# Two graph-attention layers over neighbour lists: the second layer in source order, two more row buffers, and other distances between the stages

## The chip, the cores and the metric

The kernel runs on one core of a Trainium2 chip. Its engines work beside each other, each on a queue of its own, and meet at semaphores: TensorE (PE, with its weight loads as PEld), VectorE (DVE), ScalarE (ACT), GpSimd (POOL) and SyncE (SP). POOL and SP issue the DMA transfers. The metric is the device time of one execution in microseconds (us). A profile is taken of one execution by the hardware profiler.

## The reference, cut to what matters

Two layers, each a graph attention with a residual and a layer norm. There are 8 graphs (the batch) of 2048 nodes with 256 features; all share one adjacency matrix, in which a node has 5 to 36 neighbours, itself among them.

```python
# layer 0: dot-product attention
h1, h2, h3 = x @ W1, x @ W2, x @ W3
e = leaky_relu(h1 @ h2.T, 0.2)                 # per graph, 2048 x 2048
e = where(adj > 0, e, -1e12)
x = layernorm(x + relu(softmax(e) @ h3))
# layer 1: additive attention, 4 heads of 64
q = x @ W
e = leaky_relu(q . a_src [i] + q . a_dst [j], 0.2)   # per head
e = where(adj > 0, e, -9e15)
x = layernorm(x + elu(softmax(e) @ q))
```

## The kernel before, in words

**Sparse form.** The 2048 nodes are sorted by their number of neighbours and cut into 16 tiles of 128 nodes. Tile `t` has a fixed number of neighbour slots, `SLOTS[t]`, from 36 down to 12 (596 in all). Of each tile a list of neighbour numbers is made (`neighbours`): the adjacency row, in which each entry holds its column number or 0, is cut into 24 blocks, `nc.vector.max` takes the eight largest of each block, and rounds of `max` and `match_replace` take the largest eight of what is left, until the tile's slots are filled. The lists are good if no block holds more than eight neighbours of a node; a flag is computed from the counts (`checks`), and a general path is run if it is set.

**Units.** The batch is worked in two halves of four graphs. A unit is one layer, one half and one tile; there are 64, first the 32 of layer 0 (each half from the tile of 12 slots up to that of 36), then the 32 of layer 1 (with the tile of 36 in the middle of each half). For each slot POOL gathers 128 rows, one per node, by an indirect DMA (`gather`, L203): in layer 0 from the inputs (4096 B per row: four graphs), in layer 1 from a table of projected rows that layer 0 stored (`qg`, 4160 B per row with the logit terms). Two slots make a chunk, which lies in one row buffer; there are 16 (`RING`).

**Layer 0.** `own_rows` gathers the unit's own nodes into the one buffer `xo`; `before0` copies them by four SP transfers into a residual buffer (`xr`, four of them), turns them on PE and projects them (`g`, two buffers). `logits0` takes, for each slot and graph, one fused multiply and sum on DVE (L594). Then come a softmax over the slots, diagonal matrices of the weights on ACT (`diagonals`, L723), and PE adds the rows with these as weights (`add_slot`, L706). A unit of 16 slots or more is split into two parts, each with its own softmax; the second takes the first's maximum and sum along (an online rescale). `after0` projects the sum by `W3`, adds the residual (`residual`, L778), normalises, and stores both the result and the table row for layer 1.

**Layer 1.** `logits1` adds the two logit terms per chunk (L879), `sums1` multiplies the gathered rows by the weights in place (`weighted`): four chunks of five on DVE (L943), the fifth in 32 small pieces on ACT (L939). PE sums them with a unit matrix. A unit over 24 slots, which is the tile of 36 alone, is split in two; here each part has its own maximum, and `shares` and `after1` combine both at the end (L970, L976). `after1` then makes the elu, the residual, the layer norm and scatters four blocks of rows by POOL (L211).

**What sets the order.** `tick` is called once for each slot summed, and where a stage has to wait for another. Each call advances a clock and lets every stage put a little into the queues: own rows, row gathers as far as row buffers are free (`pump`, `credits`), what has been put down for this time by `due`, diagonals up to `AHEAD` slots before the sums, and dots or adds (`stream`) up to a limit of slots before the sums. In layer 0 that limit is the slots of the next part plus `SLACK` = 9; in layer 1 it is those, plus what is left of this part, plus `LEAD` = 5. `starts`, `ends` and `lists` are queues of generators that are advanced two steps per call. For layer 0 the queues of DVE, ACT and PE are exactly in this order (`ordered`). For layer 1 that is ended (`ordered.__exit__` at unit 32), and the framework's planner orders those three engines by its own estimates of durations; POOL's order is by hand throughout, and SP's is the planner's.

**Buffers.** Sums lie in four PSUM buffers (`acc_tile`), two per part; `wide_tile` has four buffers for turned and projected rows.

Of the kernel before, what the change touches and what calls it, by code (L numbers as in the profile page):

```python
# [24 lines left out]
P = 128  # L25
# [15 lines left out]
RING = 16  # L41

SPLIT = 16
LEAD = 5
LATE = 6
SLACK = 9
AHEAD = 2

BLOCKS = 24
# [86 lines left out]
def fast_path(  # L136
# [39 lines left out]
    ring = ctx.enter_context(tc.tile_pool(name="ring", bufs=RING))  # L176
    xop = ctx.enter_context(tc.tile_pool(name="xown", bufs=1))
    xrp = ctx.enter_context(tc.tile_pool(name="xres", bufs=4))
    gp = ctx.enter_context(tc.tile_pool(name="g", bufs=2))
    wp = ctx.enter_context(tc.tile_pool(name="wide", bufs=4))  # L180
    qp = ctx.enter_context(tc.tile_pool(name="q", bufs=1))
    hsp = ctx.enter_context(tc.tile_pool(name="hs", bufs=1))
# [49 lines left out]

    twice = const.tile([P, 64], F32, tag="twice", name="twice")
# [14 lines left out]
    meta = gp.tile([P, NT, 8], F32, tag="g", name="meta")  # L248
# [4 lines left out]
    junk = hsp.tile([P, N], BF16, tag="hs", name="junk")  # L253
# [132 lines left out]
    def statistics(y, name):  # L386


        st = sp.tile([P, 2, nc.vector.BN_STATS_DIM], F32, tag="st", name=f"st_{name}")
        for i in range(2):  # L390
            nc.vector.bn_stats(st[:, i, :], y[:, 2 * i : 2 * i + 2, :].rearrange("p b c -> p c b"))  # L391
            yield
        mv = st.rearrange("p i (b s) -> p (i b) s", s=3)
        return mv[:, :, 1], mv[:, :, 2]

# [53 lines left out]
    class Unit:  # L449
        def __init__(self, layer, h, t):  # L450
# [10 lines left out]
            self.chunks = [[] for _ in self.parts]  # L461
            self.p = [None] * len(self.parts)
# [46 lines left out]
    def neighbours(t):  # L509
# [12 lines left out]
        some = sp.tile([P, 8 * BLOCKS], F32, tag="some", name=f"some_{t}", bufs=1)  # L522
        for i in range(BLOCKS):
            nc.vector.max(some[:, ts(i, 8)], v[:, N * i // BLOCKS : N * (i + 1) // BLOCKS])
            if i % 8 == 7:
                yield
# [17 lines left out]
    def own_rows(u):  # L544
        u.xo = xop.tile([P, HC], F32, tag="xo", name=f"xo_{u.name}")
        gather(u.xo, xg[u.h][:, :], order[:, u.t : u.t + 1])

    def before0(u):
# [18 lines left out]
        u.g = gp.tile([P, HC], F32, tag="g", name=f"g_{u.name}")  # L567
# [56 lines left out]
    def weights0(u, i, K, e, m):  # L624
# [7 lines left out]
        if i == len(u.parts) - 1:  # L632
# [5 lines left out]
            if i:  # L638
                due(2, spread_shares, u, e)
# [3 lines left out]
    def spread_shares(u, e):  # L643

        fs = sp.tile([P, 2, 2], F32, tag="f0", name=f"f0_{u.name}", bufs=2)
        for r in range(2):
            rr = slice(64 * r, 64 * r + 64)
            pf = ps_tile(f"ps_f0_{u.name}_{r}")[:, :2]
            for c in range(2):
# [3 lines left out]
                    rhs=e[rr, ts(c, 2), 0],  # L653
# [6 lines left out]

    def shares(u, G):


        f = sp.tile([P, 2, HG], F32, tag="f", name=f"f_{u.name}", bufs=1)[:, :, :G]
        top = sp.tile([P, HG], F32, tag="top", name=f"top_{u.name}", bufs=1)[:, :G]
        nc.vector.tensor_tensor(top, u.m[0], u.m[1], ALU.max)
        for i in range(2):
            nc.vector.tensor_tensor(f[:, i, :], u.m[i], top, ALU.subtract)
        nc.scalar.activation(f, f, AF.Exp)
        for i in range(2):  # L670
            nc.vector.tensor_tensor(u.s[i], u.s[i], f[:, i, :], ALU.mult)
        nc.vector.tensor_tensor(top, u.s[0], u.s[1], ALU.add)
        nc.vector.reciprocal(top, top)
        nc.vector.tensor_tensor(f, f, top.unsqueeze(1).to_broadcast([P, 2, G]), ALU.mult)
        fs = sp.tile([P, 2, 2, HG // 2], F32, tag="fs", name=f"fs_{u.name}", bufs=1)
        fs = fs[:, :, :, : G // 2]
        for r in range(2):
            rr = slice(64 * r, 64 * r + 64)
            pf = ps_tile(f"ps_f_{u.name}_{r}")[:, :G].rearrange("p (i g) -> p i g", i=2)
            for c in range(2):  # L680
                nc.tensor.matmul(
                    pf[64 * c : 64 * c + 64],
                    lhsT=ident[rr, rr],
# [733 lines left out]
```

## Time and profile before

| | |
|---|---|
| median of three runs | 2350.33 us (2346.8 to 2351.26) |
| the profiled execution: its time, its span | 2346.12 us, 2344.4 us |
| DVE busy | 2043.6 us (87%) |
| PE busy (weight loads) | 1714.5 us (959.1) |
| POOL busy | 1527.7 us (65%) |
| ACT busy | 1439.8 us (61%) |
| DMA | 734.95 MB, mean 313 GB/s |

A line of a group reads: line of the kernel, engine, operation, what is written and read (program names), shape, count, then busy time and the mean duration of one in ns, then the time in which the engine stood idle just before them, and what ended that. A line of waits gives the engine and line that waited, what released it, the sum in us, how often, and the longest. A line of the timeline gives start and duration in us, then the instruction, and in brackets the idle time before it and its releaser. "issue" means that the profile shows no release by another engine.

### The profile page before, as it was taken

The numbers are of one execution on the slowest core, as the hardware profiler recorded it, in microseconds if no ns is written. First come the engines' busy times: TensorE is split into PE (matmuls) and PEld (weight loads), VectorE is DVE, ScalarE is ACT, GpSimd is POOL, SyncE is SP. The second block draws the span as 40 slices with busy tenths as digits, with TensorE's granted clock in tenths as the row PEclk, the third lists the DMA queues.
The fourth block names the chain that finished last, engine by engine and source line by source line (L and its number), as shares of the span: only waits on it lengthen the run. The fifth ranks groups of instructions, "written<-read, shape, count | busy, mean of one in ns | idle before, by whom it ended". The sixth has DMA issues, their size and how long they took to land. (4 is left out here: it accounts for less than half of the span.)

```text
span 2344.4 us, 52672 instructions
## 1 busy us (share of the span) xinstructions
PE 1714.5 (73%) x16835; PEld 959.1 (41%) x16835; DVE 2043.6 (87%) x7238; ACT 1439.8 (61%) x4951; POOL 1527.7 (65%) x1485
## 2 busy tenths in 40 slices
PE   0237798898788989999998877565655776665664
PEld 0125565566455656766665532122211222222222
DVE  6587899999999987999999597888887888998996
ACT  5316577676677767888886864442564656543545
POOL 3355466665666655766776667776777777775773
PEclk9659999999999999999999988787878888887887
DMA  9877799998896889999998689978999999977992
GB/s 386 290 256 263 263 353 343 341 329 302 311 347 209 287 286 308 361 344 332 342 367 320 239 291 329 352 269 310 343 352 354 350 341 376 353 272 287 364 333 83
DMA packets 249420, 734.95 MB, mean 313 GB/s; under 512 B 63200, under 2 KB 72544, under 8 KB 246704
## 3 DMA queue, kind: packets, MB, share of 16 engines
q0 software_dynamic: 192512, 645.89, 76.4%
q1 hardware_dynamic: 55360, 84.44, 10.8%
q8 instruction: 137, 2.24, 0.4%
q10 hardware_dynamic: 1264, 1.18, 0.2%
q14 instruction: 147, 1.20, 0.1%
HBM read 708.35 MB, written 76.09 MB: 335 GB/s over the span
## 5 line engine op out<-in xcount | busy, mean ns | idle before, releaser
L594 DVE CUSTOM_DVE_ANT_0 j<-s,g 128x256 bf16<-128x256 f32 x2384 | 846.9, 420 | 57.0 <-DMA s<-xg,idx 56.4
L203 POOL DMA_INDIRECT s<-xg,idx x596 | 632.7, 1062 | 392.4 <-issue 126.8
L706 PE MATMUL acc<-s,ident 64*64 64x512 f32 x4768 | 608.9, 663 | 334.4 <-issue 277.2
L203 POOL DMA_INDIRECT s<-qg,idx x596 | 606.2, 1017 | 224.2 <-issue 132.5
L706 PE MATMUL acc<-s,dg 64*64 64x256 f32 x9536 | 632.4, 393 | 108.2 <-ACT dg L723 107.9
L723 ACT ACTIVATE dg<-twice,e 128x64 f32<-128x64 f32 x2384 | 604.4, 341 | 34.2 <-PE acc L706 16.2
L943 DVE TENSOR_TENSOR s<-s,p 128x2048 f32<-128x2048 f32 (+1 forms) x260 | 574.4, 2230 | 0.0
L706 PEld LDWEIGHTS acc<-s,ident 64*64 64x64 f32 x4768 | 209.4, 149 | 729.2 <-issue 577.6
L706 PEld LDWEIGHTS acc<-s,dg 64*64 64x64 f32 x9536 | 363.1, 136 | 334.9 <-ACT dg L723 183.2
L939 ACT ACTIVATE s<-s,e 128x64 f32<-128x64 f32 x1408 | 342.7, 335 | 47.1 <-DVE e L909 37.9
L594 DVE DVE_READ_ACCUMULATOR2_ANT e<- 128x1 f32 x2384 | 194.3, 81 | 0.0
L211 POOL DMA_INDIRECT out_dram<-o,oidx x128 | 128.7, 1006 | 68.5 <-ACT o L418 32.5
L400 ACT ACTIVATE z<-st,roots 128x4 f32<-128x4 f32 x64 | 19.0, 297 | 236.6 <-DVE st L391 202.1
L879 DVE TENSOR_TENSOR e<-s,own 128x32 f32<-128x32 f32 (+1 forms) x306 | 55.9, 186 | 104.5 <-DMA s<-qg,idx 101.9
L818 PE MATMUL ps_q<-wqs,x1T 128*128 128x264 f32 x512 | 133.4, 404 | 14.9 <-DVE y L778 14.9
L440 PE MATMUL ps_p_g<-A,xT 128*128 128x256 f32 x512 | 122.7, 393 | 1.7 <-DVE y L778 1.7
L440 PE MATMUL ps_p_h<-w_sb,hT 128*128 128x256 f32 x512 | 120.4, 388 | 2.0 <-DVE e L879 2.0
L818 PEld LDWEIGHTS ps_q<-wqs,x1T 128*128 128x128 f32 x512 | 94.1, 193 | 51.1 <-DVE y L778 17.5
L418 ACT ACTIVATE o<-xr,nmr,rstd 128x256 f32<-128x256 f32 x128 | 66.5, 589 | 75.1 <-DVE nmr L414 73.3
L1064 ACT COPY q<-ps_q 128x264 f32<-128x264 f32 x128 | 47.4, 377 | 104.1 <-PE ps_q L818 101.0
L440 PEld LDWEIGHTS ps_p_g<-A,xT 128*128 128x128 f32 x512 | 97.3, 195 | 26.3 <-issue 9.6
L440 PEld LDWEIGHTS ps_p_h<-w_sb,hT 128*128 128x128 f32 x512 | 95.1, 191 | 26.9 <-issue 14.4
(143 smaller groups left out, 1489.9 us busy)
## 6 DMA issues: line engine op xcount, KB each, us to landing
adj<-in_adj_dram SPq DMA_DIRECT2D x16, 1024.0 KB
xr<-xo SPq DMA_DIRECT2D x128, 128.0 KB
x1s<-y SPq DMA_DIRECT2D x32, 512.0 KB
xr<-x1s SPq DMA_DIRECT2D x32, 512.0 KB
s<-xg,idx POOLq DMA_INDIRECT x596
s<-qg,idx POOLq DMA_INDIRECT x596
edges<-adj SPq DMA_DIRECT2D x16, 512.0 KB
xg<-in_x_dram SPq DMA_DIRECT2D x4, 2048.0 KB
```

The costliest lines, as they stand in the source:

```text
L203: nc.gpsimd.indirect_dma_start(out=dst, out_offset=None, in_=table, in_offset=AT(ap=index, axis=0), bounds_check=table.shape[0] - 1, oob_i ...
L211: ins = nc.gpsimd.indirect_dma_start(out=table, out_offset=AT(ap=index, axis=0), in_=src, in_offset=None)
L418: nc.scalar.activation(dst[:, b, :], y[:, b, :], AF.Identity, bias=nmr[:, b : b + 1], scale=rstd[:, b : b + 1],)
L440: nc.tensor.matmul(pp[:, ts(j, C)], lhsT=srcT[:, ts((2 * i + j) * KC + k, P)], rhs=weight[:, k, :], start=(k == 0), stop=(k == KC - 1),)
L594: nc.vector.tensor_tensor_reduce(out=jt, in0=rows[:, s, ts(b, C)], in1=u.g[:, ts(b, C)], scale=1.0, scalar=0.0, op0=ALU.mult, op1=ALU.add, ...
L706: nc.tensor.matmul(out, lhsT=lhsT, rhs=rhs, start=(k == 0 and j == 0), stop=(k == K - 1 and (j == 1 or diag is None)), tile_position=(64 * ...
L723: nc.scalar.activation(diag[:, b, :], twice, AF.Copy, scale=u.p[i][:, b, k : k + 1])
L818: nc.tensor.matmul(pq[:, : C + 2 * H], lhsT=u.x1T[:, ts(i * KC + k, P)], rhs=w.sqs[:, k, j * H : j * H + CD + H], start=(k == 0), stop=(k ...
L879: nc.vector.tensor_tensor(e[:, c * CHUNK : c * CHUNK + ns, :].rearrange("p s (b g) -> p s b g", b=HB), rows[:, :ns, :].rearrange("p s (b w ...
L939: nc.scalar.activation(v[:, a, g, :], v[:, a, g, :], AF.Copy, scale=pv[:, a, g : g + 1])
L943: nc.vector.tensor_tensor(v, v, pv.unsqueeze(3).to_broadcast([P, n * HB, H, D]), ALU.mult)
L1064: heappop(events)[2]()
```

## The change

- *Lists:* the adjacency row is cut into 16 blocks for tiles of more than 19 slots and into 12 for the others, where it was 24; the rounds after that read 128 or 96 values where they read 192.
- *Row buffers:* the ring has 18 buffers. Two are held through layer 0 (`held`): one holds both `g` buffers, the other `xo` and `hs`, whose own pools are gone. They join the ring when the last table row of layer 0 has been put into POOL's queue.
- *Own rows:* a unit's own rows are gathered once the unit five before it has had its residual (`rested`), where it was at the start of the unit three before it. `before0` and `before1` of a unit start at the begin of the unit three before it, where it was in its middle.
- *Lead:* in layer 0 the dots may lead by at least 22 slots (`LEAST`); the limit was 17 to 21 for most split units. In layer 1 the limit is the slots of the next part plus 6.
- *Layer 1 in source order:* `ordered` ends after the last unit. Softmax, multiplies and ends are put down with `due` at fixed distances (`maxima1`, `weights1`, `scaled`, `share_of_first`, `after1`); the multiplies lead the sums by about two slots, the ACT pieces are spread over eight calls. A split unit is rescaled online as in layer 0: `share_of_first` scales the first part's sum after four slots of the second.

```diff
+MORE = 2
-LEAD = 5
-SLACK = 9
+SLACK = (9, 6)
+LEAST = (22, 0)
...
-    ring = ctx.enter_context(tc.tile_pool(name="ring", bufs=RING))
-    xop = ctx.enter_context(tc.tile_pool(name="xown", bufs=1))
+    ring = ctx.enter_context(tc.tile_pool(name="ring", bufs=RING + MORE))
-    gp = ctx.enter_context(tc.tile_pool(name="g", bufs=2))
-    hsp = ctx.enter_context(tc.tile_pool(name="hs", bufs=1))
...
+    held = [ring_tile(f"held_{i}") for i in range(MORE)]
+    g_rows = held[0][:, : 2 * HC].rearrange("p (i c) -> p i c", i=2)
+    xo_rows, hs_rows = held[1][:, :HC], held[1][:, HC : 2 * HC]
...
-        for i in range(BLOCKS):
-            nc.vector.max(some[:, ts(i, 8)], v[:, N * i // BLOCKS : N * (i + 1) // BLOCKS])
+        blocks = 16 if K > 19 else 12
+        for i in range(blocks):
+            nc.vector.max(some[:, ts(i, 8)], v[:, N * i // blocks : N * (i + 1) // blocks])
             if i % 8 == 7:
                 yield
...
+                if u.layer == 1:
+                    yield from scaled(u, i, K)
+                    continue
...
+    def scaled(u, i, K):
...
+        for c in range(chunks):
+            if c % SHARE == 0 and c + SHARE - 1 < chunks:
+                for a in range(operands(c + SHARE - 1, u.ps[i])[0]):
+                    due(a, by_columns, c + SHARE - 1, a)
+            n, v, pv = operands(c, u.p[i])
+            if c % SHARE != SHARE - 1:
+                nc.vector.tensor_tensor(
+                    v, v, pv.unsqueeze(3).to_broadcast([P, n, H, D]), ALU.mult
+                )
+            u.done[i] = c + 1
+            yield n // HB
...
+                rested[0] += 1
                 due(2, roots)
...
             tabled[0] += 1
+            if tabled[0] == 2 * NT:
+                credits[0] += MORE
...
+    def maxima1(u, i, k0, K, e):
...
+        if i:
+            nc.vector.tensor_copy(e[:, 0, :], u.m[0])
...
+        due(1, nc.scalar.activation, v, v, AF.Exp)
+        due(3, weights1, u, i, K, e)
...
+    def share_of_first(u):
+        u.v = wide_tile(f"v_{u.name}")[:, :HC]
+        for r in range(2):
+            nc.vector.tensor_tensor(
+                u.v[:, ts(r, HW)].rearrange("p (a d) -> p a d", d=D),
+                u.accs[0][r].rearrange("p (a d) -> p a d", d=D),
+                u.fs[:, r, :].unsqueeze(2).to_broadcast([P, HG // 2, D]),
+                ALU.mult,
+            )
...
+            for k in range(K):
+                c, s = divmod(k, CHUNK)
+                while u.done[i] <= c:
+                    yield 0
...
+                add_slot(acc, k, K, rows[:, s, :], None)
+                if s == n - 1:
+                    credits[0] += 1
+                if i == 1 and k == 4:
+                    share_of_first(u)
+                yield 1
...
+        at = 4 if split else 2
+        due(2, whole)
+        due(at, exponentials)
+        due(at + 1, below)
+        due(at + 4, less)
+        due(at + 5, above, 0)
+        due(at + 6, above, 1)
...
-        if m < min(opened[0] + 4, 2 * NT) and (m == 0 or units[m - 1].turned):
+        if m < min(rested[0] + 5, 2 * NT) and (m == 0 or units[m - 1].turned):
...
-        if j == 2 * NT:
-            ordered.__exit__(None, None, None)
...
+        if j + 3 < len(units):
+            v = units[j + 3]
+            starts.append(before[v.layer](v))
...
-            drawn[0] -= share if u.layer == 0 else 0
+            drawn[0] -= share
...
-            tick(follow[i] + (SLACK if u.layer == 0 else left - ends_of[i] + LEAD))
-            if not begun and left <= u.K / 2 and j + 3 < len(units):
...
+            tick(max(follow[i] + SLACK[u.layer], LEAST[u.layer]))
+        (after0, after1)[u.layer](u)
...
+    ordered.__exit__(None, None, None)
```

## The prediction

> **What bounds the kernel now.** I read the stage table first, then the groups by line, then what GpSimd (POOL) and VectorE (DVE) wait for in each stage, and last the order of time at the places where they stop. The profiled execution took 2346.1 us (span 2344.4); the three timed runs have a median of 2350.3, 4.2 us above it.
>
> The stage table has, per window: length, then busy time of PE, PEld, DVE, ACT and POOL, PE clock, DMA share, GB/s. Setup ends near 120, layer 0 near 1300, and the gathers of layer 1 end at 2292.
>
> ```profile
> 120.00:300.00 180.00, 115.36 (x1120) 77.39 (x1122) 149.06 (x789) 82.54 (x290) 94.16 (x89) 0.83 0.75 262
> 300.00:780.00 480.00, 418.62 (x4640) 281.29 (x4632) 464.30 (x2521) 340.19 (x1228) 306.10 (x290) 0.96 0.91 315
> 780.00:960.00 180.00, 168.22 (x1852) 117.62 (x1854) 147.93 (x789) 136.63 (x481) 107.61 (x104) 0.97 0.90 304
> 960.00:1300.00 340.00, 321.70 (x3740) 219.25 (x3736) 332.67 (x1774) 273.06 (x998) 230.96 (x218) 0.98 0.94 335
> 1440.00:2292.00 852.00, 533.14 (x4180) 182.56 (x4184) 741.17 (x997) 436.89 (x1513) 635.47 (x628) 0.81 0.91 333
> ```
>
> In layer 0 DVE is the bound: 464 of 480 and 333 of 340 us busy. It idles 31 us in 120 to 300 and 32 us in 780 to 960, where the second half of the batch begins. In layer 1 DVE is busy only 741 of 852 us. POOL's busy time, 635 of 852, looks lower, but its rows show the truth:
>
> ```profile
> 1447.35 0.99 POOL L203 DMA_INDIRECT s<-qg,idx  x1 [0.30 <-issue]
> 1448.64 0.99 POOL L203 DMA_INDIRECT s<-qg,idx  x1 [0.31 <-issue]
> ...
> 1631.66 1.44 POOL L203 DMA_INDIRECT s<-qg,idx  x1 [9.44 <-PE acc L706]
> ...
> 2151.19 0.99 POOL L203 DMA_INDIRECT s<-qg,idx  x1 [13.78 <-PE acc L706]
> ```
>
> A gather costs 0.99 us and a gap of 0.30 behind it whatever happens, 1.29 us in all, and they follow each other without a wait. 628 x 1.29 = 810 of the 852 us: POOL issues without pause, and DVE waits for it. Of what it waits for in this window
>
> ```profile
> POOL s L203 <- PE acc L706: 30.2, 25, 13.8
> DVE e L879 <- DMA s<-qg,idx: 77.7, 55, 3.4
> ```
>
> 25 waits for a free row buffer make 30.2 us, and two of them, 9.44 and 13.78, make 23.2 of it; the other 23 average 0.3, which is the gap. Both large ones follow a tile of 36 slots, the only one split in layer 1. PE shows why:
>
> ```profile
> 1627.05 18.63 PE L706 MATMUL acc<-s,ident 64*64 64x512 f32 x144 [22.93 <-issue]
> ...
> 2146.58 13.99 PE L706 MATMUL acc<-s,ident 64*64 64x512 f32 x104 [25.89 <-issue]
> ```
>
> PE stands for 22.9 and 25.9 us: a split unit holds all four sum buffers until its end combines them on DVE (L970), the next unit has none, and no rows are freed.
>
> **The change part by part.**
>
> *Lists.* Today a list takes 24 MAX8 of 85 or 86 columns, then rounds over 192 values.
>
> ```profile
> 107.90 3.60 DVE L524 MAX8 some<-nb 128x8 f32<-128x85 int16 x24
> ...
> L524 DVE MAX8 some<-nb 128x8 f32<-128x85 int16 x256 | 49.7, 231 | 0.0
> L531 DVE MAX8 m<-some 128x8 f32<-128x192 f32 x44 | 15.7, 356 | 0.3
> L533 DVE MATCH_REPLACE8 some<-m,some 128x192 f32<-128x192 f32 x28 | 9.6, 343 | 0.0
> ```
>
> From 231 ns at 85 to 356 at 192 is 1.17 ns a column. Eight in a row take 1.28 us, 160 ns each, since they overlap; so 210 ns at 128 columns and 261 at 171. A list is 3.84 us now, 16 x 0.210 = 3.36 after for the five tiles over 19 slots, 12 x 0.261 = 3.13 for the other eleven: 5 x 0.48 + 11 x 0.71 = 10.2 us. The rounds read 128 or 96 values instead of 192, 75 or 112 ns less: 29 of the 72 rounds and replacements belong to the large tiles, 43 to the others, 2.2 + 4.8 = 7.0. Together -17, all on DVE in the first half of layer 0, where it is the bound. The ends are 0 (the DMA share of 0.91 takes over) and -20.
>
> There is also one pause less or two in making a list. In 120 to 300 POOL stands five times for 10.6 to 13.4 us, each time before the first row gather of a unit, which needs its list; DVE waits 33.7 us for rows there. A pause is a slot of about 2 us, and the list is 1 us shorter: 5 x 3 = 15 us on POOL. I take -6, since DVE has other rows to work on for part of it; ends -15 and 0.
>
> *Own rows.* Before, POOL gathers them at the start of a unit, and its queue stands until the copies of the previous own rows (SP) have found a free residual buffer.
>
> ```profile
> 835.80 1.01 POOL L203 DMA_INDIRECT xo<-xg,order  x1 [8.80 <-DVE e L594]
> ...
> 844.28 0.43 DVE L594 CUSTOM_DVE_ANT_0 j<-s,g 128x256 bf16<-128x256 f32 x1 [4.87 <-DMA s<-xg,idx]
> ```
>
> Row gathers are queued behind, and DVE goes dry 8 us later; the same pair comes at 892 and 901 (6.34, then 4.52). After, the gather is put behind the residual that frees the buffer. -9 (4.87 + 4.52). At best the 8.45 us at 934, where DVE waits for a projection, goes too: -18. At worst PE, which now turns own rows some two slots after their gather in units of 12 or 13 slots, waits for the landing: four units by 2 to 3 us, +10. POOL issues and SP copies stay 32 and 128.
>
> *Lead of 22 slots and the earlier start of a unit.* The lead was 17 to 21 for most units that are split. Nothing is added; dots are moved ahead. With 32 slots of rows, those in flight fall from about 15 to 10, some 19 us of DVE against the 2.6 us that a chunk takes to issue and about 4 to land (the shortest distance from the last issue to the add that had waited for it is 4 us). I take 0. DVE idles 16 + 7 us in the stages where this acts: -16 at best. If rows run late as in 120 to 300, +25.
>
> *Layer 1 in source order.* The online rescale takes the place of the combination at the end for the two split units. The first part is scaled after four slots of the second, which frees two sum buffers before the next unit asks. Both POOL waits go: -(9.44 + 13.78 - 2 x 0.30) = -23; the other end is 0, if the next wait in line is as long. The DVE work of unsplit units (L943 at 2.28 us, adds, softmax, end) is the same; for split ones it falls by a few us, beside POOL's issues: 0. If that cover were gone, the 741 us of DVE would be the floor.
>
> What the order itself does I take as 0. An add (L879) now stands in DVE's queue with the multiplies behind it, and PE and POOL's buffers wait for those. A gap hidden until now is DVE's 111 us, of which 78 are waits for gathers. A source order that puts no add before its rows have landed gains nothing either, as POOL is the bound; at most the 20 us of buffer waits in 1300 to 1440 (25.1 less 17 gaps) go. Its bad end is the rival below.
>
> Here a rule of the Trainium skill gives another sum. Perfetto Trace Analysis, section Identifying the Most-Contended Engine, takes the engine with the highest occupancy as the one to work on, for VectorE and GpSimd alike. By it DVE (741) is ahead of POOL (635), and its idle 111 us would be what a better order can win: -111 for this part, and 2200 in all. The rows of 1447 decide against that, since POOL's gap of 0.30 us is not counted as busy and yet can't be used. Another section of that page, What "DMA-bound" means, speaks against the part in the way the rows do: where the issuing engine's track is solid DMA instructions, that engine is the bound, and no order of the other three changes it.
>
> *Two more row buffers.* They come with the last table rows, which POOL stores at 1420. After that, waits for buffers other than the two are at the gap: 0; at best part of the same 20 us.
>
> *The tail.* After the last gather (2292.4) the ends of three units follow one another. PE stands 9.06 us at 2309 for a sum buffer, and the last exponentials start 4.7 us after PE is done (2323.0, 2327.7).
>
> ```profile
> 2309.43 13.60 PE L706 MATMUL acc<-s,ident 64*64 64x512 f32 x96 [9.06 <-DVE xr L989]
> ```
>
> In source order the end of the third last is over by then, but about two chunks of the last but one are multiplied after the last adds (4.6 us): -4, ends -14 and +5.
>
> **Sum.** -17 - 6 - 9 + 0 - 23 + 0 - 4 = -59. 2346.1 - 59 = 2287; the median is mostly a little above the profiled execution, so 2288.
>
> **The rivals.**
>
> *Half of it:* one of the layers keeps its time. In layer 0 the DMA share (0.91 to 0.94) speaks for it, the 98% of DVE against it. Without layer 0's 32 us it is 2320, without layer 1's 27 us 2315. 0.20.
>
> *More of it:* the pauses at the begin of each half of layer 0 (31 + 32 us) close by two thirds instead of a quarter, 27 more, and the 20 us between the layers by half: 2288 - 37 = 2251. All of them are waits in a queue for something issued late, which is what is moved. 0.12.
>
> *Slower: adds that wait at the head of DVE's queue.* Place: L879 in layer 1, some 290 adds of two slots. POOL's solid time in that window is 852 - 23 = 829 us, DVE's work 741: waits of 88 us fit, 0.30 us an add; today's are 0.27. Beyond, the window lasts 741 us and the waits. At 0.51 us an add (147 us) it lasts 36 us longer than now, which is the gain elsewhere (32 + 4); at 0.6 us (174) it is 741 + 174 - 852 - 36 = +27: 2377. For it: adds now come 4 to 10 us after the issue, with 4 needed, so a fixed order has little room. Against it: at 20 slots a unit has 36 - 26 = 10 slots (15 us) between the issue and the add. 0.16.
>
> *No change:* the order loses in layer 1 what layer 0 gains: 2350. 0.04.
>
> **How the numbers follow.** My case has 0.48 with its own range 2265 to 2308. Faster: 0.48 + 0.20 + 0.12 = 0.80; same, within 0.2% (about what a measurement of this kernel can tell from no change, 4.7 us): 0.04; slower: 0.16. The range leaves out the slower case and the far end of the fast one: 2240 to 2345.
>
> **What would show it.** Right: no MAX8 of 85 columns, DVE in 300 to 780 still at 97% and the end of layer 0 some 32 us earlier; own-row gathers that wait under 2 us; PE without a stop over 10 us behind the 36-slot tiles, POOL at 1.29 us per gather with no wait over 3 us; at most 45 us from the last gather to the end. Wrong: POOL's waits for row buffers in layer 1 well over 30 us in many pieces, with DVE's L879 waits over 90 us (the adds), or PE waiting for own rows in the first units of a half (their gathers come too late).

## The result, and the profile after

The changed kernel takes 2434.53 us (median, 2432.91 to 2437.71) where the kernel before takes 2350.78 in the same comparison: a ratio of 1.0362, 95% interval 1.0344 to 1.038. It is 84 us slower; 62 us faster had been forecast. Its profiled execution took 2435.96 us (span 2434.1).

The span splits at three gathers of POOL. From the start to the last row gather of layer 0 it is 1304.3 us before and 1414.0 after: +109.7. From the first to the last row gather of layer 1 it is 985.7 (1305.71 to 2291.43) and 959.8 (1415.46 to 2375.24): -25.9. From there to the last scatter it is 48.5 and 54.5: +6.0. The sum, +89.8, is the difference of the spans up to the last scatter. So layer 1 gained about what was forecast for it, and layer 0 lost four times as much.

The stage table of after has the columns of the one shown for before (length; busy time of PE, PEld, DVE, ACT, POOL; PE clock, DMA share, GB/s):

```profile
120.00:300.00 180.00, 114.29 (x1090) 79.09 (x1093) 144.76 (x736) 79.66 (x278) 92.01 (x87) 0.81 0.76 261
300.00:780.00 480.00, 383.55 (x3931) 254.43 (x3924) 387.83 (x2045) 295.65 (x1050) 254.09 (x246) 0.91 0.80 278
780.00:960.00 180.00, 155.59 (x1729) 105.11 (x1728) 154.52 (x830) 123.75 (x446) 106.05 (x102) 0.92 0.79 263
960.00:1300.00 340.00, 315.90 (x3460) 215.29 (x3462) 288.89 (x1522) 258.16 (x919) 205.62 (x195) 0.98 0.91 306
1440.00:2292.00 852.00, 595.39 (x4450) 184.31 (x4450) 739.51 (x991) 455.77 (x1590) 641.12 (x632) 0.88 0.92 339
```

From 300 to 780 DVE was busy 464 of 480 us and is now busy 388; from 960 to 1300 it went from 333 to 289. It has no more work (2043.6 us in all before, 2037.1 after), it starves. Who waits for what (engine, tile, line, releaser: us in total, times, longest), over the whole of after:

```profile
DVE j L586 <- DMA s<-xg,idx: 188.4, 93, 9.0
POOL s L199 <- PE acc L668: 128.4, 107, 7.8
POOL held L199 <- DVE e L586: 79.2, 14, 9.5
POOL held L199 <- DMA xr<-held: 65.5, 9, 13.5
PE ps_t_x L422 <- DMA held<-xg,order: 63.5, 11, 14.1
```

The dots wait 188.4 us for rows (56.4 before). POOL, which issues the rows, stands at the own-row gathers (`held`): the two rows make 145 us, where the same two made 31.5 before (18.5 and 13.0; a wait of 13 us in the setup is in both). One such place, in the timeline: DVE's second residual half is done at 374.05 us and frees the residual buffer, SP issues the copies of the previous own rows into it, and POOL has put the next own-row gather directly behind.

```profile
374.08 2.65 SPq L547 DMA_DIRECT2D xr<-held  x4
```

```profile
375.92 1.10 POOL L199 DMA_INDIRECT s<-xg,idx  x1 [0.30 <-issue]
385.99 0.99 POOL L199 DMA_INDIRECT held<-xg,order  x1 [8.97 <-DMA xr<-held]
387.28 0.99 POOL L199 DMA_INDIRECT s<-xg,idx  x1 [0.30 <-issue]
```

```profile
393.19 0.42 DVE L586 CUSTOM_DVE_ANT_0 j<-s,held 128x256 bf16<-128x256 f32 x1 [5.43 <-DMA s<-xg,idx]
```

The copies are issued from 374.1 to 376.7 and land 9 us later; for those 9 us no row gather is issued, and at 387.8 DVE runs dry for 5.43 us. In the kernel before, at a like place, the own-row gather came 11 us after such copies, with seven row gathers between, and waited for nothing (the number in brackets is its gap):

```profile
359.18 2.44 SPq L555 DMA_DIRECT2D xr<-xo  x4
```

```profile
370.68 1.02 POOL L203 DMA_INDIRECT xo<-xg,order  x1 [0.30 <-issue]
```

In layer 1 the longest stop of PE for a multiply behind the first split tile, and POOL's longest wait for a row buffer between 1440 and the last gather, are

```profile
1727.55 9.97 PE L668 MATMUL acc<-s,ident 64*64 64x512 f32 x64 [6.52 <-DVE s L717]
```

```profile
1942.12 0.99 POOL L199 DMA_INDIRECT s<-qg,idx  x1 [3.34 <-PE acc L668]
```

in place of 22.93 (behind the first split tile) and 13.78 before.

### The profile page after: what moved, and what is told of

The parts are those of the page before. It is cut to its first block, busy times and chain, and to the rows that moved or that the text cites. A ratio compares the mean times of both kernels' runs of the same rounds, so it can differ in the third digit from the quotient of the medians.

```text
span 2434.1 us, 52435 instructions
## 1 busy us (share of the span) xinstructions
PE 1796.0 (74%) x16835; PEld 957.2 (39%) x16835; DVE 2037.1 (84%) x7052; ACT 1443.6 (59%) x4953; POOL 1521.4 (63%) x1485
## 5 line engine op out<-in xcount | busy, mean ns | idle before, releaser
L586 DVE CUSTOM_DVE_ANT_0 j<-s,held 128x256 bf16<-128x256 f32 x2384 | 850.4, 419 | 189.5 <-DMA s<-xg,idx 188.4
L668 PE MATMUL acc<-s,ident 64*64 64x512 f32 x4768 | 649.1, 681 | 291.0 <-DVE s L717 250.2
L199 POOL DMA_INDIRECT s<-xg,idx x596 | 625.8, 1050 | 369.1 <-issue 151.2
L668 PE MATMUL acc<-s,dg 64*64 64x256 f32 x9536 | 657.9, 401 | 110.5 <-ACT dg L688 109.4
L668 PEld LDWEIGHTS acc<-s,dg 64*64 64x64 f32 x9536 | 371.3, 139 | 354.3 <-ACT dg L688 193.8
L668 PEld LDWEIGHTS acc<-s,ident 64*64 64x64 f32 x4768 | 185.1, 149 | 747.3 <-DVE s L717 426.6
L707 ACT ACTIVATE s<-s,e 128x64 f32<-128x64 f32 x1408 | 349.9, 335 | 91.9 <-DVE e L922 50.3
L1081 ACT ACTIVATE e<-e 128x40 f32<-128x40 f32 (+21 forms) x88 | 27.8, 316 | 314.9 <-DVE e L898 182.2
L199 POOL DMA_INDIRECT held<-xg,order x32 | 34.4, 1076 | 181.5 <-DVE e L586 79.2
L430 PE MATMUL ps_p_g<-A,xT 128*128 128x256 f32 x512 | 128.4, 406 | 22.0 <-ACT xT L1081 9.4
L430 PEld LDWEIGHTS ps_p_g<-A,xT 128*128 128x128 f32 x512 | 100.5, 202 | 49.4 <-ACT xT L1081 10.3
L430 PEld LDWEIGHTS ps_p_h<-w_sb,hT 128*128 128x128 f32 x512 | 96.6, 194 | 25.9 <-issue 13.2
```

Source lines behind the costliest of these rows:

```text
L199: nc.gpsimd.indirect_dma_start(out=dst, out_offset=None, in_=table, in_offset=AT(ap=index, axis=0), bounds_check=table.shape[0] - 1, oob_i ...
L430: nc.tensor.matmul(pp[:, ts(j, C)], lhsT=srcT[:, ts((2 * i + j) * KC + k, P)], rhs=weight[:, k, :], start=(k == 0), stop=(k == KC - 1),)
L586: nc.vector.tensor_tensor_reduce(out=jt, in0=rows[:, s, ts(b, C)], in1=u.g[:, ts(b, C)], scale=1.0, scalar=0.0, op0=ALU.mult, op1=ALU.add, ...
L668: nc.tensor.matmul(out, lhsT=lhsT, rhs=rhs, start=(k == 0 and j == 0), stop=(k == K - 1 and (j == 1 or diag is None)), tile_position=(64 * ...
L707: nc.scalar.activation(v[:, a, g, :], v[:, a, g, :], AF.Copy, scale=pv[:, a, g : g + 1])
L1081: heappop(events)[2]()
```

## The experiments

Layer 0 has three changed steps that move the order of work: the gate of the own rows (`rested`), the lead of at least 22 slots, and the earlier start of a unit. The theories: the gate is the main cause, since POOL stops behind it; the lead is, since rows wait longer in their buffers between dot and sum, so that fewer buffers are left for rows in flight; or DVE's work or the layer's other changes are. Where a run's time is set beside another's, both ran on chips on which the kernel before takes 2350 to 2352 us.

### e1, the gate put back

```diff
-        if m < min(rested[0] + 5, 2 * NT) and (m == 0 or units[m - 1].turned):
+        if m < min(opened[0] + 4, 2 * NT) and (m == 0 or units[m - 1].turned):
```

(`opened[0] = j` stands at the start of unit j again.)

> The changed kernel with one condition put back: a unit's own rows are gathered at the start of the unit three before it, not behind the residual. Theory Q (queue): in the changed kernel the own-row gather stands in GpSimd's queue right behind the residual; it may not overwrite the own-row buffer before SyncE's four copies of the previous rows are through, those wait for that same residual, and the row gathers queued behind stand still. Its GpSimd waits at own rows are about 180 us, 52 before. Q expects them to fall to 40 to 70 us, DVE's waits for layer 0 rows from 188 to under 90, and the time to 2300 to 2350. Theory L (lead): with dots 22 slots ahead too few rows are in flight; it expects 2400 to 2434. Theory S (start): the earlier start of a unit makes PE turn own rows before they have landed (64 us of PE waits); it expects 2390 to 2434.

Measured: 2434.41 us, ratio 1.0361 (1.0331 to 1.0391), the time of after. The waits changed hands:

```profile
POOL s L199 <- PE acc L668: 289.6, 165, 7.9
PE ps_t_x L422 <- DMA held<-xg,order: 167.5, 26, 14.9
DVE j L586 <- DMA s<-xg,idx: 117.3, 86, 8.1
```

POOL no longer stands at own rows but 289.6 us for row buffers, and PE stands 167.5 us for own rows that land too late for a unit that starts early. So the gate is not the main cause: with the lead and the early start beside it, it costs nothing that can be measured.

### e2, the lead taken back

```diff
-LEAST = (22, 0)
+LEAST = (0, 0)
```

> The changed kernel without the least lead of 22 slots in layer 0 (slots of the next part plus 9, as before). Q expects 2415 to 2440, since GpSimd's stops at own rows stay. L expects DVE's waits for layer 0 rows to fall from 188 to about 60 us and the time to 2320 to 2360.

Measured: 2343.59 us, 0.9973 (0.9959 to 0.9987). This one constant is 91 us of the changed kernel. What is left of the waits:

```profile
DVE j L586 <- DMA s<-xg,idx: 107.4, 54, 8.1
POOL held L199 <- DVE e L586: 76.8, 14, 8.9
POOL held L199 <- DMA xr<-held: 70.7, 10, 13.1
```

POOL stands at own rows as long as in after (147.5 us against 144.7), but DVE waits for rows 54 times instead of 93 (36 in the kernel before): with more rows in flight, it works through more of them.

### e3, the start of a unit put back

```diff
-        if j + 3 < len(units):
-            v = units[j + 3]
-            starts.append(before[v.layer](v))
+            if not begun and left <= u.K / 2 and j + 3 < len(units):
+                begun = True
+                v = units[j + 3]
+                starts.append(before[v.layer](v))
```

> The changed kernel with a unit started in the middle of the unit three before it, as before, not at its begin. S expects PE's waits for own rows to fall from 64 to about 30 us and the time to 2340 to 2380. Q expects 2420 to 2450: the copies wait for the residual in either case, and the gather for the copies.

Measured: 2429.03 us, 1.0317 (1.0296 to 1.0339). PE's waits for own rows fall from 63.5 to 29.3 us, what they were before, and the time by 5 us: beside the lead and the gate, what PE waited for was not what cost the time.

### e4 and e6, the gate alone and the lead alone in the kernel before

```diff
-        if m < min(opened[0] + 4, 2 * NT) and (m == 0 or units[m - 1].turned):
+        if m < min(rested[0] + 5, 2 * NT) and (m == 0 or units[m - 1].turned):
```

(The counter `rested` of the change comes with it.)

> The kernel before with one condition of the change alone: own rows behind the residual of the unit five before. Q expects that this alone costs most of it: 2410 to 2460, with 120 to 200 us of GpSimd waits at own rows. L and S expect 2340 to 2365.

```diff
-            tick(follow[i] + (SLACK if u.layer == 0 else left - ends_of[i] + LEAD))
+            tick(max(follow[i] + SLACK, 22) if u.layer == 0 else follow[i] + left - ends_of[i] + LEAD)
```

> The kernel before with the least lead of 22 slots alone. Theory L (the lead keeps row buffers occupied, and the way from a freed buffer over gather and landing to the dots no longer fits into the buffers that are left) needs nothing else of the change: 2415 to 2460, with GpSimd's waits for row buffers (164 us) over 250. If the lead hurts only together with held buffers, shorter lists or the early start: 2340 to 2375.

Measured: the gate alone 2377.09 us, 1.0099 (1.0073 to 1.0126), +26; the lead alone 2392.60, 1.0177 (1.0158 to 1.0196), +42. The prediction had -9 and 0 for them. Both times lie between the ranges of the theories: each step costs alone, and neither costs alone what it was said to. POOL's waits at own rows with the gate alone (a wait of 11 us in the setup, the same in the kernel before, is left out):

```profile
POOL xo L203 <- DVE e L594: 47.3, 9, 9.0
POOL xo L203 <- PE acc L706: 38.8, 6, 9.5
POOL xo L203 <- DMA xr<-xo: 26.4, 5, 13.4
POOL xo L203 <- PE ps_p_g L440: 25.6, 4, 6.9
```

and with the lead alone:

```profile
POOL s L203 <- PE acc L706: 169.6, 121, 13.7
DVE j L594 <- DMA s<-xg,idx: 108.1, 72, 6.5
```

The gate makes 138 us of stops where there were 31.5. What ends a stop is named differently from one to the next; in the place shown for after it is the landing of the copies. With the lead POOL's waits are nearly those of before (164.1 for buffers), not the 250 that the theory of the lead named, but DVE's waits for rows nearly double from 56.4. Worked out from the times of the records (end of a row gather to the slot's first dot, last dot to its last sum matmul, medians over layer 0): before, 11.5 and 37.0 us; lead alone 8.9 and 42.0; after 8.1 and 44.9. A slot of layer 0 takes 1.99 us before ((1304 - 120) / 596) and 2.17 after, so 19 of the 32 slots of rows are held between dot and sum before and 21 after, and rows come 3 us nearer to their use. If all 32 are in use, the round of a row buffer is 32 times the time of a slot: 64 us before, 66 with the lead alone, 70 after. What the two medians leave of it, some 15, 15 and 16.5 us, lies between a slot's last sum and the end of the gather that fills its place again (an estimate, since medians are subtracted).

### e5, lead and gate taken back; e9, the start as well

> The changed kernel without the least lead of 22 and with own rows at the start of a unit, as before: layer 1, the shorter lists, the held buffers and the early start of a unit are left. By theory L the lead costs about 90 us, by Q the own-row gather 26 us more once the lead is gone; both together: 2343.6 - 26 = 2318, between 2295 and 2325. If Q's cost is hidden behind something else of the change: 2335 to 2350.

> The changed kernel with all three of its new distances in layer 0 put back (lead, own rows, start of a unit); layer 1, lists and held buffers are left. Theory S+ (own rows at the start of a unit and a unit that starts there too bring PE's turning right behind the gather; PE's waits for own rows were 30 us before, 64 in the changed kernel, 102 without lead and gate) expects PE's waits at 25 to 45 us and 2300 to 2318, the end of layer 0's sums 15 to 25 us earlier than the 1362 us of the run without both. If the early start is harmless: 2325 to 2337.

Their edits are those of e2 and e1, and of e2, e1 and e3. Measured: 2331.10 us, 0.9927 (0.9908 to 0.9946), and 2313.86, 0.9837 (0.9817 to 0.9858). So, without the lead, the gate costs 12.5 us (e2 less e5) and the early start 17 (e5 less e9: PE's waits for own rows 101.5 against 31.2 us). e5 itself lies between its two ranges. The lead costs 103 with the early start alone (e1 less e5). What is left in e9 is layer 1, the lists and the shared buffers, and its split is the forecast's shape: layer 0 ends at 1294.2 (-10.1), layer 1's gathers take 957.0 us (-28.7), the tail 53.9 (+5.4), together -33.4 against -33.5 in the spans.

### e7 and e10, two buffers not counted; e11, two buffers taken away

```diff
-    credits = [RING]
+    credits = [RING - 2]
...
-                credits[0] += MORE
+                credits[0] += MORE + 2
```

The edit is made on e5 (e7) and on e9 (e10).

> As the run without both, but with two of the sixteen row buffers left unused until layer 0 is over; the lead is the old one. Theory L counts slots: four slots less are as bad as four slots more of lead, and layer 0 gets 60 to 120 us longer: 2380 to 2440. If the larger lead costs by the order it gives to DVE, ACT and PE and not by buffers: within 15 us of the run without both.

> As that, with two of the sixteen row buffers of layer 0 not counted as free, so that a gather takes a buffer freed two chunks ago and need not wait for the sum just put down; all sixteen stay in rotation. Where the early start stood this won 18 us. If it won by sparing GpSimd's queue the wait for PE (194 us of waits for buffers there, 78 with it): another 5 to 18 us, 2290 to 2310, waits for buffers under 110. If it only repaired what the early start had spoilt: within 4 us of the run with all three.

Measured: e7 2313.21 us, 0.9845 (0.9823 to 0.9867), 18 us faster than e5; e10 2308.30, 0.9808 (0.9787 to 0.983), 6 us faster than e9 and the fastest here. It is the opposite of what fewer buffers should do, and by the code there were not fewer. The count in the planner fell, but all 16 stayed in rotation, so that by the code a gather is put down two chunks later and takes a buffer that was freed two chunks earlier. POOL's waits for buffers fall, e9 first, then e10:

```profile
POOL s L199 <- PE acc L668: 154.0, 122, 11.4
```

```profile
POOL s L199 <- PE acc L668: 73.4, 98, 5.3
POOL held L199 <- DMA xr<-held: 48.1, 8, 13.3
POOL held L199 <- PE acc L668: 35.8, 4, 12.8
```

But they have only turned into stops at own rows: worked out from the records between 130 us and the last row gather of layer 0, POOL stands at own rows 133 us in e10 and 34 in e9, and is idle 430 us in both. In e10 22 of these stops are over 1 us, up to 12.8, 130 us in all, as many as with the gate alone (24, up to 9.5, 130 us), and it is the fastest kernel here. So time in which POOL stands at own rows is not by itself a loss; the reading that fits is that in e10 the rows behind would have waited for a buffer in any case. What the 6 us come from was not tested.

In e11 two buffers are really gone in layer 0:

```diff
+    taken = [ring_tile(f"taken_{i}") for i in range(2)]
+    for r in taken:
+        nc.gpsimd.memset(r[:, 0:1], 0.0)
...
+                for r in taken:
+                    nc.gpsimd.memset(r[:, 0:1], 0.0)
```

> As that, but two buffers are really taken out of the rotation through layer 0, so fourteen are left; the order of all work is the same. Only layer 0 is to be compared. Theory L (rows held between dot and sum leave too few buffers for gather and landing) expects the last sum of layer 0 to be 30 to 100 us later and DVE's waits for rows over 110 us. If buffers are not what the larger lead runs out of: within 10 us.

Measured: 2384.25 us, 1.0128 (1.01 to 1.0156): 76 us more than e10, all of it in layer 0 (last row gather at 1369.6 against 1290.7).

```profile
DVE j L589 <- DMA s<-xg,idx: 138.8, 84, 8.2
POOL s L199 <- PE acc L671: 213.0, 131, 10.5
```

These are waits like those of the kernels with the lead, with no lead in it, and rows come nearer to their use as there: from the end of a row gather to the first dot it is 8.3 us at the median, 10.3 in e10, while from dot to sum it is 37.3 and 35.9. Two buffers are four slots of rows: that layer 0 has hardly any to spare is shown. That a longer lead takes them in the same way is the reading that fits the 8.9 and 8.1 us of above; the other theory, that the lead costs by the order it gives to DVE, ACT and PE, would be settled by a run with the lead and more buffers, which was not made.

### e8, own rows behind the residual, but later

On e2:

```diff
-        if m < min(rested[0] + 5, 2 * NT) and (m == 0 or units[m - 1].turned):
+        if m < min(len(rested) + 5, 2 * NT) and (m < 5 or rested[m - 5] + 6 <= clock[0]) and (m == 0 or units[m - 1].turned):
```

(`rested` collects the clock of the residuals; it goes up by one with each `tick`.)

> The changed kernel without the least lead, and with the own-row gather behind the residual of the unit five before by six calls of the planner more. Q says that only the nearness to the residual and to the copies that wait for it costs: 2300 to 2325, GpSimd's waits at own rows under 60 us. If the gate itself (own rows four units ahead) costs, for example by PE turning rows late: 2335 to 2350, as with the gate right behind the residual.

Measured: 2370.73 us, 1.0081 (1.0062 to 1.01), 27 us more than e2, and above both ranges. Six calls of `tick` later POOL's stops at own rows in layer 0 are gone, but for 2.2 us, and

```profile
PE ps_t_x L422 <- DMA held<-xg,order: 107.5, 17, 13.9
DVE y L772 <- PE ps_p_h L430: 59.9, 13, 17.1
```

PE waits for own rows instead (57.2 us in e2), and DVE for PE (6.5 in e2). Between too early for the copies and too late for PE there is little room for a gather tied to the residual.

### e12, lists from 24 blocks

On e9:

```diff
-        blocks = 16 if K > 19 else 12
+        blocks = 24
```

(with `some` of 192 columns again.)

> As the run with all three distances put back, but lists from 24 blocks again. The prediction gives the shorter lists 17 us of DVE work and 6 us of earlier rows: 15 to 25 us slower than that run. If row transfers bound the first half of layer 0: within 5 us.

Measured: 2325.13 us, 0.9881 (0.9858 to 0.9904). The shorter lists are worth 11 us, where the step had 23 and the run 15 to 25. The work went as forecast: DVE is busy with lists for 88.4 us in e12 and 70.4 in e9. The pauses went further: POOL stands 77.5 us before the first row gathers of the units of the first half in e12, 45.0 in e9. But that freed nothing for DVE: it is idle for 70 us of layer 0 in both (all three worked out from the records, layer 0 from 130 us to the last row gather). In the profiled executions layer 0 ended 15 us earlier (1309.2 and 1294.2).

### Chips of another kind: e13 to e18

The last runs came to three other chips, on which the kernel before takes 2604, 2602 and 2576 us. There PE stands much longer without a wait that the profile shows. The weight loads of e9, and of e14, which is the same in layer 0, over the whole kernel:

```profile
PEld acc L668 <- issue: 313.0, 826, 4.1
```

```profile
PEld acc L669 <- issue: 821.4, 1497, 6.8
```

Why is not known. Times from these chips are set only beside each other.

e13 is e9 with the lead put in again, e16 the same kernel on the second chip:

```diff
-LEAST = (0, 0)
+LEAST = (22, 0)
```

> The kernel with the three steps put back (lists, layer 1 and buffers of the change; 2313.9), and the lead of at least 22 slots in it again. Alone in the kernel before the lead cost 42 us, in the changed kernel 91 to 103. Theory A, the lead is made dearer by the two steps that let POOL or PE stand (own rows behind the residual, start of the third next unit): here, without them, it costs about 42, so 2350 to 2365, and the last sum of layer 0 near 1385. Theory B, it is dearer because of what came with the rest of the change (shorter lists, buffers held for other uses): 80 or more here, so 2395 to 2415, last sum of layer 0 above 1425.

> The same kernel as the run before it that put the lead back alone (three steps put back, then the lead of at least 22 in again), wanted on a chip on which the kernel before takes 2350 us and not 2604. The theories as there: the lead made dearer by own rows and early start (A): 2350 to 2365 at 2350 of before, a ratio of 1.000 to 1.006; made dearer by the lists and the held buffers (B): 2395 to 2415, a ratio above 1.019. If the chip is again one of 2604, it stands beside the run before: a ratio near 0.9905.

e14 is e9 with the two row buffers that come free for layer 1 kept out of use, from the last table rows to the end:

```diff
-                credits[0] += MORE
+                for i in range(MORE):
+                    taken.append(ring_tile(f"taken_{i}"))
+                    nc.gpsimd.memset(taken[i][:, 0:1], 0.0)
...
+    for r in taken:
+        nc.gpsimd.memset(r[:, 0:1], 0.0)
```

> The kernel with the three steps put back (2313.9), but the two row buffers that come free with the last table rows stay out of use in layer 1, which has 16 as before. By the prediction's step (POOL issues without a pause there, the two are worth nothing) within 5 us of 2313.9. If layer 1 is as close to its number of buffers as layer 0 (two buffers fewer cost 76 us there): 2340 or more, with POOL waits for buffers of 40 us and more between 1440 and the last gather.

e15 is e10 with a shorter lead, and e17 the same on the second chip:

```diff
-SLACK = (9, 6)
+SLACK = (6, 6)
```

> The fastest of the kernels so far (2308.3: three steps put back, two buffers of layer 0 kept uncounted) with the lead in layer 0 made shorter: 6 slots beyond the part that follows, where the kernel before has 9 and the change 22 in all. If the slots of lead cost by the buffers that they hold, and 9 is already past the best, POOL's waits for row buffers fall under 60 us and the time to 2290 to 2303. If 9 is needed to have the weights of a part ready when its turn comes, PE waits for weights and the time rises to 2315 to 2335.

> The same kernel as the run with 6 slots of lead beyond the part that follows, wanted on a chip on which the kernel before takes 2350 us. If the slots of lead cost by the buffers that they hold, it is under 2303, a ratio under 0.980; if 9 slots are needed to have the weights ready, 2315 to 2335, a ratio of 0.985 to 0.993.

e18 is the changed kernel as it stands, on the third:

> The changed kernel as it stands, wanted on a chip of the kind on which the kernel before takes 2602 us. There, the kernel with the lead of at least 22 but without own rows behind the residual and without the early start took 2577 (ratio 0.989), and layer 0 of the same kernel without the lead was no shorter (last row gather at 1448 us without, 1429 and 1436 with). Theory A, the lead is dear only together with those two steps: 2640 to 2680, a ratio of 1.014 to 1.03, last row gather of layer 0 after 1500. Theory B, they add no more than they cost without the lead (13 to 30 us on the other chips): 2590 to 2607, a ratio of 0.995 to 1.002. On a chip on which the kernel before takes 2350 it is a repeat: a ratio of 1.036.

| run | before there | us | ratio (interval) | last row gather of layer 0 | layer 1's gathers |
|---|---|---|---|---|---|
| e14, no lead, 16 buffers in layer 1 | 2603.6 | 2598.9 | 0.998 (0.9958 to 1.0001) | 1447.8 | 1087.8 |
| e13, lead | 2603.6 | 2576.4 | 0.9905 (0.9888 to 0.9921) | 1428.6 | 1071.4 |
| e15, shorter lead | 2603.6 | 2590.7 | 0.9961 (0.9945 to 0.9978) | 1452.1 | 1068.9 |
| e16, lead | 2602.3 | 2576.8 | 0.9888 (0.9855 to 0.992) | 1436.2 | 1075.1 |
| e17, shorter lead | 2602.3 | 2594.2 | 0.997 (0.9951 to 0.9988) | 1457.6 | 1071.9 |
| e18, all of the change | 2576.3 | 2624.5 | 1.0181 (1.013 to 1.0232) | 1498.5 | 1056.3 |

With PE slow the lead alone is no loss: layer 0 of e13 and e16 is 12 to 19 us shorter than that of e14. There PE is late by itself (last dot to last sum 48.3 us at the median in e14, without the lead, and 50.9 in e13), so the buffers are held in any case. With own rows behind the residual and the early start beside it, layer 0 is 62 to 70 us longer than with the lead alone, though on that chip the kernel before is 26 us faster, and the waits of after are back (first e18, then e16):

```profile
DVE j L586 <- DMA s<-xg,idx: 158.6, 84, 9.6
POOL held L199 <- DMA xr<-held: 62.1, 9, 13.4
```

```profile
DVE j L586 <- DMA s<-xg,idx: 99.6, 73, 7.7
```

By the ratio that is theory A's side, on this kind of chip (the last row gather, at 1498.5, is just short of its 1500): the lead is dear together with the steps that make POOL or PE stop. On chips like those of the result, e9 with the lead alone was not measured, so how the 121 us between e9 and after divide there among lead, gate and start stays open, beyond the pairs above. In layer 1 the two added buffers are worth 16 us here (1087.8 against 1071.4 on the same chip), where the prediction had 0. With the shorter lead (and two buffers not counted) layer 0 is 4 to 10 us longer than e14's; e10 itself was not run here, and what the shorter lead does on the other kind isn't known.

## Why the prediction was wrong

| step | predicted, us | measured, us | from |
|---|---|---|---|
| lists, and rows earlier by them | -17 - 6 | -11 (list work of DVE -18) | e12 to e9 |
| own rows behind the residual | -9 (-18 to +10) | +26 alone; in the changed kernel +12.5 without the lead, 0 with it | e4; e5 to e2; e1 to after |
| lead of 22 and earlier start | 0 (-16 to +25) | lead +42 alone, +91 and +103 in the changed kernel; start +17, and +5 beside lead and gate | e6; e2 to after, e5 to e1; e9 to e5, e3 to after |
| layer 1: online rescale and order | -23 | -25.9 (-28.7 in e9) | gathers of layer 1 |
| two more row buffers | 0 | not measured; 16 us on the other kind of chip | e14, e13 |
| tail | -4 (-14 to +5) | +6 | last gather to last scatter |

**The step that failed first is the cost of the lead**: "those in flight fall from about 15 to 10, some 19 us of DVE against the 2.6 us that a chunk takes to issue and about 4 to land", and "I take 0". The slots held between dot and sum were about right, 21 of 32. But the rest are not all in flight. At 1.99 us a slot, the 11.5 us from the end of a gather to the dot are under six slots before, where the step had 15; the 8.1 us of after, at 2.17, are under four, where it had ten. The other seven or eight are the 15 to 16.5 us between the last sum and the next gather's end, which the step left out. By the code, a buffer comes free only when PE has summed both its slots, a part with an odd number of slots leaves half a buffer empty, a list in the making has one of the sixteen, and the gather waits in POOL's queue behind everything else there. The landing was taken too short as well: about 4 us is the shortest, and the rows that DVE waited for, the late ones, landed 5.9 us after the end of their gather at the median (3.4 to 9.7, after; 6.2 before). Against these, the margin is about 2 us after and 5 before. A stop of POOL of 9 us, as at 377 to 386, is then 5 us of idle DVE, and POOL stops at the own rows of 24 of the 32 units for over 1 us, up to 9.5. I had priced the waiting time of one transfer, not the whole round from sum to gather to landing to dot, and e11 shows what is left over in that round: less than four slots.

**The second is the own rows.** The -9 removed a stop seen at 835.80, and the step put the gather directly behind the residual. What frees the target there is not the residual but SP's copies, which only begin with it: 2.65 us of issue and about 9 to land, all at the head of POOL's queue. The bad end that I gave, +10, looked at PE alone. How much of its +26 alone are these stops is not shown, as e10 has as many and loses nothing; DVE's waits for rows went from 56.4 to 81.8 us with it. **The third** is the early start at nothing: gathered at the same time, own rows are late for it (101.5 us of PE waits in e5).

The three don't just add up, as e18 beside e16 shows on the other chips; that they draw on the same margin is the reading that fits. After is 121 us above e9, where the gate and the lead alone, in the kernel before, cost 68 and the start 17. What is left without the three had been forecast at -50 (lists, layer 1, tail) and came to -38 in e9.

**Right** was layer 1, in the mechanism. POOL at 1.29 us a gather was its bound, and the two stops behind the split tiles went: -23. That the sum is so near, -25.9, is partly luck. Worked out from POOL's gaps over 0.30 us, the stops in the first 80 gathers fell by another 9 us, and new small ones made 10: POOL's waits for buffers are 32.8 us in 47 pieces between 1440 and 2375, of which none is over 3.4. And four scatters fewer, a unit's, lie before the last gather (108 of 128, 112 before), which shortens this stretch and puts them into the tail; from the first row gather to the last scatter it is 1034.2 us before and 1014.3 after, -19.9 where -27 was forecast. By the Trainium skill, Perfetto Trace Analysis, section Identifying the Most-Contended Engine, DVE with the higher occupancy would have been the engine to relieve there. The prediction's other sum made its idle 111 us the prize; between 1440 and 2292 DVE was busy 741 us before and 740 after, and the gathers took 26 us less, 22 of them POOL's stops. The rival with the slower end put its loss there, too (L879, at 2377), in the wrong layer: DVE's waits for rows in that add went from 77.7 us (1440 to 2292) to 99.4 (1440 to 2375), beside POOL's issues. Of the signs named for a wrong outcome some came, small: these waits are over the 90 named, POOL's waits for buffers there are many pieces and just over 30 us, and PE waited for own rows 14.1 us at 234 and 8.4 at 922, among the first six units of a half. None of them holds the loss: layer 1 got shorter, and with PE's waits gone in e3 the time fell by 5 us. What shows it is the first of the right signs, DVE at 97% in 300 to 780: it was at 81%.

The lists gave half of what was forecast, though DVE's work on them fell by 18 us, where the sum had 17, and POOL's pauses by 32, where it had 15 (e12). The -6 for earlier rows was not there, as DVE is idle as long in both; what took the rest is not shown. The tail has the opposite sign, within 1 us of the bad end given; a part of it are the four scatters.

## What to carry to other kernels

How far one engine may run ahead of another is paid in buffers: before lengthening a lead, count slots for the whole round (last use, release, reissue, landing, first use), and see how many us a row is there before it is used, against the longest stop of the engine that issues. A transfer that is put into an in-order queue directly behind the event that starts the clearing of its target waits for the whole clearing, and everything behind it with it; see what work can stand between, and that the reader of the target can wait that long, which it could not in e8. Before a stop in a trace is called a loss, ask whether what stands behind it could have gone earlier: in e10 it costs nothing. Steps that each look free in a tight stage should be priced together, as they may draw on the same margin.

## What was not expected of the hardware

The same kernel took 2350 us on two chips and 2576 to 2604 on three others, at a granted clock that is no lower there: 0.875 to 0.884 in the runs of before beside e1 to e12, 0.882 to 0.897 in those beside e13 to e18. There a matmul of the sums of layer 0 took as long (401 ns in e13, 395 in e9), but PE stood for weight loads with nothing to wait for 207.5 us in 428 pieces in layer 0 of e13, against 24.4 in 114 in e9. Whether that is the chip or something else of those runs is not shown. On these chips the lead put into e9 was no loss; on the others it costs 42 us in the kernel before. And four copies of 128 KB between buffers of the core took 9 us to land, after 2.65 us of issue (374.08 to 385.99), as long as seven row gathers take to issue.
